# exp(scores) times V in a graph-attention layer: each matmul made as two of 64 queries, in two column tiles

## The chip, the core and the metric

The kernel runs on one core of a Trainium2 chip, everything in 32-bit floating point. The metric is the device time of one execution in microseconds (us), the median of several runs. A core has a tensor engine (PE, whose weight loads the profile lists apart as PEld), a vector engine (DVE), a scalar engine (ACT), GpSimd (POOL) and a queue that issues transfers (SP). Matmuls write to PSUM, the memory that DVE and ACT read the results from.

## The reference

128 graphs of 128 nodes, 768 features, 12 heads of 64. Cut to what matters:

```python
h = jnp.maximum(_layernorm(x), 0.0)
q = _split_heads(h @ Wq + bq); k = _split_heads(h @ Wk + bk); v = _split_heads(h @ Wv + bv)
scores = jnp.einsum('bhqd,bhkd->bhqk', q, k) / jnp.sqrt(HD) + beta * adj_e
scores = jnp.where(adj_e > 0, scores, -9e15)
probs = softmax(scores, axis=-1)
out = x + jnp.einsum("bhqk,bhkd->bhqd", probs, v)      # b: 128 graphs; heads put side by side
```


## The kernel before, in words

The work goes in 32 groups G of four graphs. A group needs three projections, called slices: `qk0` (queries and keys of heads 0 to 5), `v`, and `qk1` (queries and keys of heads 6 to 11). A slice is made of 15 products (`product`, line 316 is its matmul), by a scheme of sums and differences of blocks that needs fewer products than the plain one. Each product is 4 matmuls in the code, of 128 stationary columns and 256 moving columns, accumulated in one of four PSUM banks a, b, c, d; in the trace each matmul of the code is two weight loads and two matmuls, so a product is a group of 8. The very first slice is made in the plain way (`plain_slice`, line 443).

Attention works on pairs of heads; `oc` (0 to 5) numbers the pair. `scores(G, oc)` (matmul in line 355) makes the scores of both heads for the group's four graphs, keys on the partitions, queries along the free dimension. Its matmuls contract over 64 partitions: head i = 0 uses partitions 0 to 63 and i = 1 uses 64 to 127, two row tiles of the tensor engine's array, and the innermost loop alternates between them. DVE then caps the scores and adds the bias (line 358), ACT takes exp (line 359), and the results stand in the tiles `es[G, oc, i]` (called e in the trace).

`attend(G, oc)` (line 379) multiplies them with V: for each half r of the group, two graphs g and two heads i, exp(scores) of a graph and head, 128 keys by 128 queries, is the stationary operand; the moving operand is V of that graph and head, 128 keys by 65 columns, whose 65th column is ones, so that the sum of each row comes along. The result, 128 queries by 65, goes into a PSUM tile `pa` (called av in the trace) that holds four of them. A call is 8 matmuls in the code, 16 in the trace. `weigh` (lines 364 to 370) divides by the sums on DVE, POOL adds x (line 383), and SP writes the result out.

Each engine carries out its instructions in the order in which they are written. That order is written by hand: `slice_of` makes the products one after the other and calls, after certain products, the functions of a list `todo`. `attention(G, u)` fills it for three pairs of heads:

```python
for i in range(3):
    todo.setdefault(1 + 4 * i, []).append(lambda oc=3 * u + i: scores(G, oc))
    todo.setdefault(5 + 4 * i, []).insert(0, lambda oc=3 * u + i: attend(G, oc))
```

so scores stand after products 1, 5 and 9, attends after 5, 9 and 13, and after products 5 and 9 attend comes directly ahead of the next scores. Pairs 0 to 2 of a group are attended in its own `qk1` slice, pairs 3 to 5 in the next group's `qk0` slice. In the last group all six pairs have to be finished in its `qk1` slice: three calls of `attend` after products 3, 6 and 9, each followed by scores, and then six calls of `attend_half` (line 411), which do half the graphs each, directly behind calls of `scores_half` (line 397). All PSUM tiles of attention come from one ring of four banks (tag "at"), those of the products from another (tag "mm").

The kernel ends with a test of ranges (line 579 is its matmul), on which a second, plain computation (`general`) depends that isn't taken here.

Of the kernel before, what the change touches and what calls it, by code (L numbers as in the profile page):

```python
# [16 lines left out]
P = 128  # L17
# [89 lines left out]
def direct(ctx, tc, x, adj, wq, bq, wk, bk, wv, bv, beta, out, bad):  # L107
# [10 lines left out]
    nc = tc.nc  # L118
    B, N, D = x.shape
    HD = D // HEADS  # L120
# [17 lines left out]
    xg, A, biasT, vt, qk = {}, {}, {}, {}, {}  # L138
# [204 lines left out]
    es, xo = {}, {}  # L343
# [17 lines left out]
    def weigh(G, oc, r, pa, o):  # L361

        sm = stat.tile([P, 4, 1], F32, tag="sm", name=f"sm_{G}_{oc}_{r}")
        nc.vector.tensor_scalar(sm, pa[:, :, HD:VE], TINY, None, op0=ALU.max)
        rs = stat.tile([P, 4, 1], F32, tag="rs", name=f"rs_{G}_{oc}_{r}")
        nc.vector.reciprocal(rs, sm)
        nc.vector.tensor_mul(o, pa[:, :, 0:HD], rs.to_broadcast([P, 4, HD]))  # L367
        for i, t in enumerate((sm, rs)):
            s = seen[:, i, 4 * r:4 * r + 4]
            nc.vector.tensor_tensor(s, s, t.rearrange("p b e -> p (b e)"), ALU.max)  # L370

    def attend(G, oc):
        o = work.tile([P, 2, 4, HD], F32, tag="o", name=f"o_{G}_{oc}", bufs=2)
        for r in range(2):
            pa = psum.tile([P, 4, VE], F32, tag="at", name=f"av_{G}_{oc}_{r}")
            for g in range(2):
                for i in range(2):
                    h = 2 * oc + i
                    nc.tensor.matmul(pa[:, 2 * g + i, :], es[G, oc, i][:, 2 * r + g, :],  # L379
                                     vt[G, "v", r, h // 4][:, 4 * g + h % 4, :], start=True, stop=True)  # L380
            weigh(G, oc, r, pa, o[:, r])
        t = xo[G, oc]
        nc.gpsimd.tensor_add(t, t, o.rearrange("p a (b j) d -> p (a b) (j d)", j=2))  # L383
        nc.sync.dma_start(out[G * GRP:(G + 1) * GRP, :, oc * P:(oc + 1) * P].rearrange("g n d -> n g d"), t)
# [20 lines left out]
    def attend_half(G, oc, r):  # L405
        o = work.tile([P, 4, HD], F32, tag="o", name=f"o_{G}_{oc}_{r}", bufs=2)
        pa = psum.tile([P, 4, VE], F32, tag="at", name=f"av_{G}_{oc}_{r}")
        for g in range(2):
            for i in range(2):
                h = 2 * oc + i  # L410
                nc.tensor.matmul(pa[:, 2 * g + i, :], es[G, oc, r][:, i, g, :],  # L411
                                 vt[G, "v", r, h // 4][:, 4 * g + h % 4, :], start=True, stop=True)
        weigh(G, oc, r, pa, o)
        t = xo[G, oc, r]
        nc.vector.tensor_add(t, t, o.rearrange("p (b j) d -> p b (j d)", j=2))
        g0 = G * GRP + 2 * r
        nc.sync.dma_start(out[g0:g0 + 2, :, oc * P:(oc + 1) * P].rearrange("g n d -> n g d"), t)

    def attention(G, u):

        todo = {}
# [3 lines that stand above are left out]
        return todo  # L425
# [72 lines left out]
    for G in range(NG):  # L498
# [64 lines left out]
        for at, f, *args in (  # L563
            (0, scores, 0), (3, attend, 0), (3, scores, 1), (6, attend, 1), (6, scores, 2), (9, attend, 2),
            (9, scores_half, 5, 0), (10, scores_half, 4, 0), (11, attend_half, 5, 0), (12, scores_half, 3, 0),
            (12, attend_half, 4, 0), (13, scores_half, 3, 1), (13, attend_half, 3, 0), (14, scores_half, 5, 1),
            (14, attend_half, 3, 1), (14, scores_half, 4, 1), (14, attend_half, 5, 1), (14, attend_half, 4, 1),
        ):
            then(at, lambda f=f, args=args: f(G, *args))
# [143 lines left out]
```

## Time and profile before

| | |
|---|---|
| median of three runs | 3119.64 us (3119.45 to 3120.21) |
| profiled execution | 3119.99 us |
| its span, first to last instruction | 3118.2 us |
| granted clock of the tensor engine | 0.999 |
| HBM traffic | 54 GB/s over the span |

A row of the profile's groups names the line, the engine, the operation, the output and input tiles, for the tensor engine the rows and columns of the array in use (128*128, or 64*128 for the scores), the shape, and the count; then the busy time in us and the mean duration of one in ns, and last the idle time of the engine ahead of them. A busy time counts overlapping instructions once, and a matmul's duration holds its way through the array, so it is longer than the step from one matmul to the next. In the timeline, rows of equal instructions are merged: start, duration of the whole, engine, line, operation, tiles, shape and count. A row of one line's instructions gives the least, the median and the largest duration in ns.

### The profile page before, as it was taken

The page shows a single profiled execution, that of the slowest core. Times are in us where ns is not written, and L with a number is a line of the kernel's source. Part 1 is how long each engine was busy: PE and PEld are TensorE (multiplying, and loading weights), DVE is VectorE, ACT ScalarE, POOL GpSimd, SP SyncE. Part 2 cuts the span into 40 slices and gives each one's busy share as a digit, 9 for nine tenths or more (in the row PEclk, how much of TensorE's full clock was granted, in tenths as well). Part 3 has the DMA queues.
Part 4 walks back from the last instruction along what each step waited for, and adds up shares of the span by engine and source line. Part 5 has one row for each costly group of instructions (what it writes and reads, how often), then busy time and mean ns, then how long its engine had stood idle before and what let it go on. Part 6 is the DMA issues. An engine that isn't in the chain of part 4 may idle for free.

```text
span 3118.2 us, 46382 instructions
## 1 busy us (share of the span) xinstructions
PE 3099.8 (99%) x17846; PEld 2748.6 (88%) x17846; DVE 2000.8 (64%) x5155; ACT 801.1 (26%) x1703; POOL 375.8 (12%) x307
## 2 busy tenths in 40 slices
PE   8999999999999999999999999999999999999999
PEld 7888888888888888888888888888888888888887
DVE  7866656666566665666656666556666566665654
ACT  2222222322222222222232222222322222222221
POOL 1111111011110111111111111111011110111110
PEclk9999999999999999999999999999999999999999
DMA  5212112121122121221112212112121122111111
GB/s 154 72 48 58 41 48 65 52 54 46 44 65 58 48 55 42 57 62 49 54 40 56 65 48 58 41 48 65 52 55 44 46 65 57 49 52 40 56 35 38
DMA packets 358481, 169.94 MB, mean 54 GB/s; under 512 B 84464, under 2 KB 358128, under 8 KB 358256
## 3 DMA queue, kind: packets, MB, share of 16 engines
q1 hardware_dynamic: 355392, 166.14, 19.4%
q8 instruction: 142, 2.33, 0.3%
q10 hardware_dynamic: 2864, 0.79, 0.1%
q14 instruction: 83, 0.68, 0.1%
HBM read 116.53 MB, written 50.33 MB: 54 GB/s over the span
## 4 chain that ended last, share of the span: by engine, by line
PE 98%; DVE 1%; DMA 0%; ACT 0%; issue 0%; SPq 0%; ACTq 0%; DVEq 0%
PE pc_qk L316 18%; PE pb_qk L316 14%; PE pa_qk L316 14%; PE av L379 10%; PE pc_v L316 9%; PE pb_v L316 7%; PE pa_v L316 7%; PE pd_qk L316 7%; PE sc L355 7%; PE pd_v L316 4%; PE plain L443 1%; DMA x<-in_x_dram 0%; ACT x L259 0%; DVE A L266 0%; PE av L411 0%; PE pm L228 0%
## 5 line engine op out<-in xcount | busy, mean ns | idle before, releaser
L383 POOL TENSOR_TENSOR xo<-xo,o 128x512 f32<-128x512 f32 x189 | 258.3, 1367 | 2427.1 <-DVE seen L370 1496.1
L359 ACT ACTIVATE e<-e 128x512 f32<-128x512 f32 x378 | 231.9, 630 | 752.3 <-DVE e L358 751.6
L259 ACT ACTIVATE x<-x,shift,rstd 128x192 f32<-128x192 f32 x512 | 228.0, 533 | 588.3 <-POOL shift L250 588.3
L379 PEld LDWEIGHTS av<-v,e 128*128 128x128 f32 x3024 | 367.4, 192 | 9.8
L316 PE MATMUL pb_qk<-S,qk_T 128*128 128x256 f32 x1512 | 367.1, 386 | 0.0
L379 PE MATMUL av<-v,e 128*128 128x65 f32 x3024 | 358.2, 272 | 0.0
L337 ACT ACTIVATE qk<-pc_qk,bqk 128x256 f32<-128x256 f32 x378 | 158.1, 469 | 727.6 <-PE pc_qk L316 727.6
L358 DVE SCALAR_TENSOR_TENSOR e<-sc,biasT 128x512 f32<-128x512 f32 x378 | 243.0, 685 | 127.0 <-PE sc L355 127.0
L316 PEld LDWEIGHTS pb_qk<-S,qk_T 128*128 128x128 f32 x1512 | 277.3, 190 | 40.1
L341 DVE TENSOR_TENSOR qk<-qk,pb_qk 128x512 f32<-128x512 f32 x252 | 172.1, 683 | 162.9 <-PE pb_qk L316 144.7
L316 PE MATMUL pc_qk<-S,qk_B 128*128 128x256 f32 x1008 | 244.7, 386 | 1.2 <-ACT qk L337 1.2
L316 PE MATMUL pa_qk<-S,qk_T 128*128 128x256 f32 x1008 | 244.8, 386 | 0.0
L316 PE MATMUL pc_qk<-S,qk_T 128*128 128x256 f32 x1008 | 238.1, 379 | 0.0
L266 DVE STREAM_TRANSPOSE A<-x 128x256 f32<-128x256 f32 x384 | 217.4, 612 | 7.4 <-ACT x L259 7.3
L355 PE MATMUL sc<-qk 64*128 64x128 f32 x3024 | 219.6, 285 | 0.0
L316 PEld LDWEIGHTS pc_qk<-S,qk_T 128*128 128x128 f32 x1008 | 191.5, 190 | 26.0
L316 PEld LDWEIGHTS pc_qk<-S,qk_B 128*128 128x128 f32 x1008 | 186.3, 190 | 31.9 <-ACT qk L337 1.6
L316 PEld LDWEIGHTS pa_qk<-S,qk_T 128*128 128x128 f32 x1008 | 186.2, 190 | 30.5
L355 PEld LDWEIGHTS sc<-qk 64*128 64x128 f32 x3024 | 183.4, 187 | 29.5 <-issue 20.9
L316 PE MATMUL pb_v<-v_T,S 128*128 128x256 f32 x768 | 183.9, 382 | 0.0
L341 DVE TENSOR_TENSOR qk<-qk,pd_qk 128x512 f32<-128x512 f32 x126 | 86.6, 688 | 147.3 <-PE pd_qk L316 147.3
L367 DVE TENSOR_TENSOR o<-av,rs 128x256 f32<-128x256 f32 x384 | 160.3, 418 | 2.3 <-DVE seen L370 0.4
(117 smaller groups left out, 4516.1 us busy)
## 6 DMA issues: line engine op xcount, KB each, us to landing
x<-in_x_dram SPq DMA_DIRECT2D x504, 96.0 KB, 2.4
xo<-in_x_dram SPq DMA_DIRECT2D x189, 256.0 KB, 2.8
out_dram<-xo SPq DMA_DIRECT2D x189, 256.0 KB, 2.2
adj<-in_adj_dram SPq DMA_DIRECT2D x128, 64.0 KB, 2.3
qk_T<-in_L_gnn_Wq_dram SPq DMA_DIRECT2D x10, 128.0 KB, 3.2
qk_T<-in_L_gnn_Wk_dram SPq DMA_DIRECT2D x10, 128.0 KB, 3.1
v_T<-in_L_gnn_Wv_dram SPq DMA_DIRECT2D x5, 256.0 KB, 5.7
qk_B<-in_L_gnn_Wq_dram SPq DMA_DIRECT2D x8, 128.0 KB, 3.1
```

Source lines behind the costliest of these rows:

```text
L259: nc.scalar.activation(t, t, AF.Relu, bias=shift[G, n], scale=rstd[G, n])
L266: last = nc.vector.transpose(t[:, :, g * N:(g + 1) * N].rearrange("p c (b i) -> p c b i", i=SQ), src)
L316: nc.tensor.matmul(p[:, i, :], lhs, rhs, start=(first and i == 0 and c == 0), stop=(c == 1), skip_group_check=True)
L337: nc.scalar.activation(t[:, i, :], p[:, i, :], AF.Identity, bias=bqk[:, i, oc:oc + 1], scale=float(sign))
L341: added[G] = nc.vector.tensor_tensor(t, t, p, ALU.add if sign > 0 else ALU.subtract)
L355: nc.tensor.matmul(ps[i][:, g, :], t[r, 1, at], t[r, 0, at], start=True, stop=True)
L358: nc.vector.scalar_tensor_tensor(e, ps[i], SCORE_CAP * ISCALE, biasT[G], op0=ALU.min, op1=ALU.add)
L359: nc.scalar.activation(e, e, AF.Exp, scale=1.0 / ISCALE)
L367: nc.vector.tensor_mul(o, pa[:, :, 0:HD], rs.to_broadcast([P, 4, HD]))
L379: nc.tensor.matmul(pa[:, 2 * g + i, :], es[G, oc, i][:, 2 * r + g, :], vt[G, "v", r, h // 4][:, 4 * g + h % 4, :], start=True, stop=True)
L383: nc.gpsimd.tensor_add(t, t, o.rearrange("p a (b j) d -> p (a b) (j d)", j=2))
L443: nc.tensor.matmul(p[:, i, :], b[:, c, i * P:(i + 1) * P], a[:, c, :], start=(k == 0 and i == 0 and c == 0), stop=(c == 1), skip_group_che ...
```

## The change

In `attend` and `attend_half` each matmul becomes two, for queries 0 to 63 and 64 to 127 (`P` is 128, `HD` is 64). The stationary operand of each has 64 columns; the output goes to partitions 0 to 63 or 64 to 127 of the same PSUM tile, which puts the matmul on columns 0 to 63 or 64 to 127 of the array, two column tiles with all 128 rows each. The moving operand, V with 65 columns, is the same for both.

```diff
                 for i in range(2):
                     h = 2 * oc + i
-                    nc.tensor.matmul(pa[:, 2 * g + i, :], es[G, oc, i][:, 2 * r + g, :],
-                                     vt[G, "v", r, h // 4][:, 4 * g + h % 4, :], start=True, stop=True)
+                    for q in range(0, P, HD):
+                        nc.tensor.matmul(pa[q:q + HD, 2 * g + i, :], es[G, oc, i][:, 2 * r + g, q:q + HD],
+                                         vt[G, "v", r, h // 4][:, 4 * g + h % 4, :], start=True, stop=True)
             weigh(G, oc, r, pa, o[:, r])
```

The edit in `attend_half` is the same, with `es[G, oc, r][:, i, g, q:q + HD]` as the stationary operand.

More of the change, by code (lines that the diff above doesn't have):

```diff
@@ L410, in attend_half @@
                 h = 2 * oc + i
-                nc.tensor.matmul(pa[:, 2 * g + i, :], es[G, oc, r][:, i, g, :],
-                                 vt[G, "v", r, h // 4][:, 4 * g + h % 4, :], start=True, stop=True)
+                for q in range(0, P, HD):
+                    nc.tensor.matmul(pa[q:q + HD, 2 * g + i, :], es[G, oc, r][:, i, g, q:q + HD],
+                                     vt[G, "v", r, h // 4][:, 4 * g + h % 4, :], start=True, stop=True)
         weigh(G, oc, r, pa, o)
```

## The prediction, made before the change was run

> **What bounds the kernel now.** I read the page from the top: the busy times, then the chain of work that ended last, then the costliest groups, and after that the waits of the tensor engine.
>
> ```profile
> span 3118.2 us, 46382 instructions
> PE 3099.8 (99%) x17846; PEld 2748.6 (88%) x17846; DVE 2000.8 (64%) x5155; ACT 801.1 (26%) x1703; POOL 375.8 (12%) x307
> PEclk9999999999999999999999999999999999999999
> PE 98%; DVE 1%; DMA 0%; ACT 0%; issue 0%; SPq 0%; ACTq 0%; DVEq 0%
> L379 PEld LDWEIGHTS av<-v,e 128*128 128x128 f32 x3024 | 367.4, 192 | 9.8
> L379 PE MATMUL av<-v,e 128*128 128x65 f32 x3024 | 358.2, 272 | 0.0
> L355 PE MATMUL sc<-qk 64*128 64x128 f32 x3024 | 219.6, 285 | 0.0
> ```
>
> The tensor engine (PE) runs without a gap at its full clock, and the chain is PE for 98%. The other engines are never what ends last, so a microsecond taken from PE is a microsecond off the end, until some engine behind it falls late. The waits of PE say how near that is:
>
> ```profile
> engine line waited for: us in total, times, longest us
> PE pm L228 <- DVE st L219: 7.2, 2, 5.8
> ...
> PE pc_qk L316 <- ACT qk L337: 1.2, 1, 1.2
> ```
>
> The two largest lines are shown; all waits together are 13.4 us of 3118, and most of them stand at the start. The change touches the two groups named av: 3024 weight loads and 3024 matmuls, 16 of each per call of attend (each matmul of the code is two instructions in the trace), so 189 calls, and a matmul with 65 moving columns. What sets the pace inside such a call is read from the timeline of PE and of its weight loads (PEld). Columns: start, duration, engine, line, count.
>
> ```profile
> 1532.68 1.89 PE L316 MATMUL pa_qk<-S,qk_T 128*128 128x256 f32 x8
> 1534.40 1.90 PE L379 MATMUL av<-v,e 128*128 128x65 f32 x16
> 1536.23 1.16 PE L355 MATMUL sc<-qk 64*128 64x128 f32 x16
> 1537.32 1.99 PE L316 MATMUL pc_qk<-S,qk_B 128*128 128x256 f32 x8
> 1539.15 1.89 PE L316 MATMUL pb_qk<-S,qk_T 128*128 128x256 f32 x8
> ...
> 1554.26 1.90 PE L379 MATMUL av<-v,e 128*128 128x65 f32 x16
> 1555.99 0.43 PE L316 MATMUL pb_qk<-S,qk_T 128*128 128x256 f32 x1
> ```
>
> ```profile
> 1532.46 1.70 PEld L316 LDWEIGHTS pa_qk<-S,qk_T 128*128 128x128 f32 x8
> 1534.19 1.97 PEld L379 LDWEIGHTS av<-v,e 128*128 128x128 f32 x16
> ```
>
> ```profile
> L379 PE MATMUL av<-v,e x3024: 220/275/275, 87.2 to 3090.6; 128*128 128x65 f32 x189
> L316 PE MATMUL pc_qk<-S,qk_T x1008: 379/379/379, 75.6 to 3072.4; 128*128 128x256 f32 x168
> ```
>
> A product's 8 matmuls of 256 columns hold PE for 1.72 to 1.73 us until the next group (1532.68 to 1534.40), 0.216 us each, and their loads, which begin 0.22 us ahead of the matmuls they serve, vanish under the matmul before. The streaming price of a column comes from the shortest durations in the last fence: (379 - 220) / (256 - 65) = 0.83 ns, so 65 columns stream in 54 ns. Yet 16 av matmuls hold PE for 1.73 us until the next group (1554.26 to 1555.99). Their 16 loads take 1.97 us from first start to last end; the first lies under the product's last matmul, 0.216 us ahead of the second, and the 14 steps that are left make (1.97 - 0.19 - 0.216) / 14 = 0.112 us from load to load. So av is bound by its weight loads: 128 columns of exp(scores) take 0.112 us, and the 54 ns of streaming lie under the next load. The median av matmul is 275 ns against 220: 55 ns of waiting for weights, the other half of 0.112.
>
> **The load of 64 columns.** The trace has one load of another width, the last matmul of the kernel with one column:
>
> ```profile
> L579 PEld LDWEIGHTS pf<-over,ones x2: 79/80/82, 3112.3 to 3112.3; 128*1 128x1 f32 x2
> ```
>
> 192 - 80 = 112 ns for 127 columns more, 0.88 ns a column: 64 columns fewer shorten a load by 56 ns, to 56 ns of pace. Half of 0.112 says the same. The matmul beside it, 54 ns of streaming plus 3 ns (0.216 us of L316 less 256 x 0.83 ns), has a pace of 57 ns. I take p = 0.058 us for one load and one matmul on one column tile, the larger plus the trace's 10 ns rounding over the block.
>
> **Do two tiles run at once?** No column tile is in this trace; the nearest row is the scores, which use two row tiles (64*128). Their 16 matmuls stream 128 columns, 128 x 0.83 = 106 ns each, with a load of 128 columns each, 0.112 us. One after the other would be 1.79 us; from 1536.23 to 1537.32 they take 1.09 us, and that contains a change of mode. Between the ends stand: full overlap, p = 0.058 us for each pair of tiles, and none, 2 x 0.058 = 0.116 us. I take full overlap, since the row tiles show it in fp32, with the same alternation of tiles from one matmul to the next as the new inner loop over q, and since the two new matmuls write different partitions of a bank.
>
> On this the Trainium skill, page "TensorE: Matmul & The Clock Gate", section "Part 3: Packing small matmuls — row/col tiling", gives a measured 2.38 times for three column tiles. My estimate from that page is 2.38 / 3 x 2 = 1.59 for two, hence p = 0.112 / 1.59 = 0.070 us, and a total of 3040 us by the formula below; no run here shows it.
>
> **The change of mode, which is added.** Between full-array matmuls and the scores PE changes its tiling. What that costs is read from starts: a product takes 8 x 0.216 = 1.73 us, but
>
> ```profile
> 1524.48 1.89 PE L316 MATMUL pa_qk<-A,qk_T 128*128 128x256 f32 x8
> 1526.30 1.16 PE L355 MATMUL sc<-qk 64*128 64x128 f32 x16
> 1527.39 1.99 PE L316 MATMUL pb_qk<-S,qk_T 128*128 128x256 f32 x8
> 1529.22 1.89 PE L316 MATMUL pc_qk<-S,qk_T 128*128 128x256 f32 x8
> ```
>
> the product ahead of the scores holds PE for 1.82 us: 0.09 us in which the array empties. The product behind them has 1.99 instead of 1.89 us and lasts 1.83: 0.10 us in which its first load stands exposed. The scores themselves close: 0.10 exposed + 8 x 0.112 + 0.09 = 1.09 us, the measured value. So a mode change costs 0.09 us plus the first load; for a 64-column load I take half, 0.05 us.
>
> **The sum for one call of attend.** Today, from its first matmul to the next group's: 1.83 us where the scores follow (1534.40 to 1536.23), 1.73 us where a product follows, and there the product's first matmul has 0.05 us of waiting for weights (0.43 against 0.38 us), so 1.78. Afterwards: 0.09 to empty the array ahead of it (new, since a product comes before), 0.05 for the first load, 16 p = 0.93 for 16 pairs, 0.09 to empty it again, 1.16 us together. The scores behind it pay for their exposed load today already. A product behind it now pays 0.10: 1.26.
>
> So 0.67 us are saved where the scores follow and 0.52 where a product follows. The order is the same for every slice of attention: attends at places 5, 9 and 13, scores at 1, 5 and 9, so two calls of three are followed by scores. The last group's first three (LAST) are all followed by scores. That gives 62 calls with a product behind and 127 with scores, 189 in all. 127 x 0.67 + 62 x 0.52 = 117 us. As a formula in p, for use below: saved = 127 (1.60 - 16 p) + 62 (1.45 - 16 p) = 293 - 3024 p, with 118 us at p = 0.058 (the difference is rounding).
>
> The six half calls at the end (L411) are taken at nothing: 48 instructions, at most 48 x 0.054 = 2.6 us, in a tail where exp ends some of the waiting.
>
> **What could be late next.** attend reads exp(scores), which the vector and scalar engines finish well before:
>
> ```profile
> 1538.11 1.28 DVE L358 SCALAR_TENSOR_TENSOR e<-sc,biasT 128x512 f32<-128x512 f32 x2
> 1538.88 1.23 ACT L359 ACTIVATE e<-e 128x512 f32<-128x512 f32 x2 [3.44 <-DVE e L358]
> ...
> 1526.00:1587.00 61.00, 61.00 (x384) 54.13 (x383) 42.65 (x117) 17.04 (x35) 7.36 (x6) 1.00 0.23 66
> ```
>
> The av that reads these tiles starts four products later, and exp ends at 1540.11, when one of the four products has passed (1537.32 to 1539.15) and the second has run 0.96 us; over 4 us remain, and the products that carry this margin are unchanged. In the stretch of attention slices (third line: PE, PEld, DVE, ACT, POOL) DVE has 42.65 of 61 us; with six calls less 0.6 us each, 42.65 of 57.2, 75%. No queue gains an instruction but PE's (3072 loads and 3072 matmuls more), no DMA is added, and no semaphore wait by the code. If DVE's cover went, each bank handed back late would cost PE its length; nothing in the waits of PE points there.
>
> The profiled execution took 3119.99 us, 1.8 beyond its span; the runs shown have a median of 3119.64. 3119.99 - 118 = 3002 us.
>
> **Rivals.** *The tiles take turns.* If the loads of both column tiles pass one path into the array, a pair costs 2 x 0.058 = 0.116 us, no more than 128 columns cost today, and the mode changes are pure loss: 293 - 3024 x 0.116 = -58, 3178 us. It decides from p = 293 / 3024 = 0.097 us on. For it: both tiles read the same 128 partitions, while the row tiles of the scores read disjoint ones. Against it: loads and matmuls already read the same partitions at once (PEld 1532.46 under PE). 0.10.
>
> *A load may not pass a matmul of the other tile.* Then a pair is 0.058 of loading and 0.057 of streaming in turn, 0.115 us: 3175 us. The trace speaks against the mechanism where it can be seen, since the L316 loads run under matmuls of the same 128 rows; it has no case with tiles on the same rows. 0.06. The Trainium skill has this rule, in the same section of "TensorE: Matmul & The Clock Gate": a load overlaps matmuls in flight only if its row group differs, and the two column tiles have the same rows. By that rule the change would lose; the L316 rows above disagree with it in its plain form.
>
> *Instructions come too slowly.* The densest stretch today is the scores, 32 instructions in 8 x 0.112 us, 0.028 us each; the new call wants 0.0145. Held to 0.028, a pair with its four instructions costs 0.112: 3166 us. Nothing shows 0.028 to be a limit, because the loads set that pace by themselves. 0.02.
>
> *No tiling happens.* The narrow matmuls run one after the other in the full array, without mode changes: 32 x 0.058 against 16 x 0.112, 0.07 us more per call, 189 x 0.07 = 13, 3133 us. For it: the label 128*1 of the last load names the columns in use, not a tile. Against it: the row tiles came from the operands' partitions alone. 0.05.
>
> *Break-even*, p near 0.097 within 0.002: 0.03.
>
> **How the numbers follow.** Full overlap 0.74, the others 0.26. 0.2% of the time is 6 us, about what a measurement of this kernel can tell from no change; only the break-even case lies inside it. Faster 0.74, same 0.03, slower 0.10 + 0.06 + 0.02 + 0.05 = 0.23. The likeliest case's own range: below, if entering the column tiles needs no emptying (189 x 0.09 = 17 us) nor leaving them for a product (62 x 0.09 = 6): 2980. Above, if a mode change with column tiles costs twice as much (189 x 0.14 + 62 x 0.19 = 38 us): 3040, and 3045 with some late banks. The whole range reaches on to the untiled case, 2980 to 3135, and leaves out the three serial ones, 0.18.
>
> **What would show it.** In the changed profile the av rows should read 128*64 with 6048 of each kind, loads of about 136 ns. A call should run 1.0 us in the timeline, with starts of matmuls in pairs; the next group begins 1.07 us after the first av matmul, and the product ahead lasts 1.82 us. The chain stays PE for 98%, with av near 6%. A call of about 2 us means turns or a limit of issue; a call of 1.8 us with no 0.09 us ahead of it means no tiling; calls of 1.1 us with a saving far under 118 us mean that DVE became late, to be seen as waits of PE for L332, L341 or L367. The prediction is wrong if p is over 0.072 us.

## The result, and the profile after

The changed kernel takes 3007.57 us (median of four runs, 3005.77 to 3007.84) against 3119.86 us before (3119.45 to 3120.21, four runs). The ratio is 0.9639, 95% interval 0.9622 to 0.9656: 112 us less, where 118 were forecast. The page of the profile after, with the rows that answer to those of before:

```profile
span 3006.0 us, 52526 instructions
...
PE 2985.7 (99%) x20918; PEld 2579.4 (86%) x20918; DVE 1996.6 (66%) x5155; ACT 797.3 (27%) x1703; POOL 359.7 (12%) x307
...
PE 98%; DVE 1%; DMA 0%; ACT 0%; issue 0%; SPq 0%; ACTq 0%; DVEq 0%
...
L380 PEld LDWEIGHTS av<-v,e 128*64 128x64 f32 x6048 | 192.6, 138 | 62.9 <-issue 43.0
...
L380 PE MATMUL av<-v,e 128*64 128x65 f32 x6048 | 218.8, 225 | 0.0
```

PE still fills 99% of the span, and the chain is PE for 98%: no other engine became the bound. The av rows read 128*64, so the tiles were made, with twice the instructions (6048) in 219 instead of 358 us of busy time. A load of 64 columns takes 138 ns against 192, near the 136 that the one-column load had led to expect. A matmul's mean is 225 ns against 272: close to the 220 ns that it takes without a wait, so the waiting for weights is nearly gone. The idle time ahead of these loads grew from 9.8 to 62.9 us, which is 0.33 us in each of the 189 calls: the first load of a call, which started 0.21 us ahead of its matmul before (1534.19 and 1534.40), now starts together with it (both 1483.19 below), 0.09 us after the product ahead has had its 1.73.

The timeline of PE after shows two calls with what stands around them, the first followed by scores, the second by a product. Columns: start, duration, engine, line, count.

```profile
1481.37 1.89 PE L316 MATMUL pa_qk<-S,qk_T 128*128 128x256 f32 x8
1483.19 1.16 PE L380 MATMUL av<-v,e 128*64 128x65 f32 x32
1484.27 1.16 PE L355 MATMUL sc<-qk 64*128 64x128 f32 x16
1485.37 2.00 PE L316 MATMUL pc_qk<-S,qk_B 128*128 128x256 f32 x8
```

```profile
1440.37 1.89 PE L316 MATMUL pa_qk<-S,qk_B 128*128 128x256 f32 x8
1442.19 1.15 PE L380 MATMUL av<-v,e 128*64 128x65 f32 x32
1443.27 2.00 PE L316 MATMUL pb_qk<-S,qk_T 128*128 128x256 f32 x8
1445.10 1.89 PE L316 MATMUL pc_v<-v_T,S 128*128 128x256 f32 x8
```

Ahead of av the product now holds PE for 1.82 us in place of 1.72, the added change of mode. The call itself takes 1.08 us to the next group's start; before it took 1.83 ahead of scores and 1.73 ahead of a product. Behind it the product now lasts 1.83 us (1443.27 to 1445.10), with its first load exposed. A row merges the matmuls of a group; their single starts, which the trace holds too, fall in 16 pairs in each of the 189 calls, the second of a pair 7 ns (median) behind the first. The waits of PE after:

```profile
engine line waited for: us in total, times, longest us
PE pm L228 <- DVE st L219: 7.1, 2, 5.8
PE pc_qk L316 <- ACT qk L337: 2.3, 1, 2.3
PE plain L445 <- DVE A L266: 2.0, 1, 2.0
PE pf L581 <- DVE over L578: 1.7, 1, 1.7
PE av L413 <- ACT e L404: 0.9, 2, 0.5
PE pm L243 <- DVE dev L235: 0.5, 1, 0.5
```

They add up to 14.5 us. Before, the six lines (7.2, 1.7, 1.6, 1.2, 0.5 and 0.2 us) make 12.4, and not the 13.4 of the prediction: 2.1 us more, in the first 97 us and at the end. Behind the longest of the waits that grew (2.3 us, up to 97.38), the clock granted to PE is 0.50 from about 98.8 to 102.2 us, which the profile before does not have. The call of `attend` there takes 1.93 us in place of 1.08. My estimate is 1.7 us of lost time, half of these 3.4.

### The profile page after: what moved, and what is told of

Its sections match the earlier page's. It is cut to its first block, busy times and chain, and to the rows that moved or that the text cites. A ratio compares the mean times of both kernels' runs of the same rounds, so it can differ in the third digit from the quotient of the medians.

```text
span 3006.0 us, 52526 instructions
## 1 busy us (share of the span) xinstructions
PE 2985.7 (99%) x20918; PEld 2579.4 (86%) x20918; DVE 1996.6 (66%) x5155; ACT 797.3 (27%) x1703; POOL 359.7 (12%) x307
## 4 chain that ended last, share of the span: by engine, by line
PE 98%; DVE 1%; DMA 0%; ACT 0%; issue 0%; SPq 0%; ACTq 0%; DVEq 0%
PE pc_qk L316 18%; PE pb_qk L316 15%; PE pa_qk L316 15%; PE pc_v L316 9%; PE pb_v L316 7%; PE pa_v L316 7%; PE pd_qk L316 7%; PE av L380 7%; PE sc L355 7%; PE pd_v L316 4%; PE plain L445 1%; DMA x<-in_x_dram 0%; ACT x L259 0%; DVE A L266 0%; DVE qk_T L199 0%; PE pm L228 0%
## 5 line engine op out<-in xcount | busy, mean ns | idle before, releaser
L384 POOL TENSOR_TENSOR xo<-xo,o 128x512 f32<-128x512 f32 x189 | 242.1, 1281 | 2330.5 <-DVE seen L370 2300.9
L380 PEld LDWEIGHTS av<-v,e 128*64 128x64 f32 x6048 | 192.6, 138 | 62.9 <-issue 43.0
L380 PE MATMUL av<-v,e 128*64 128x65 f32 x6048 | 218.8, 225 | 0.0
L272 DVE TENSOR_TENSOR S<-A,A 128x512 f32<-128x512 f32 x224 | 164.2, 747 | 1.0
```

The costliest lines, as they stand in the source:

```text
L272: nc.vector.tensor_tensor(t, A[G, a], A[G, b], ALU.add if sign > 0 else ALU.subtract)
L380: nc.tensor.matmul(pa[q:q + HD, 2 * g + i, :], es[G, oc, i][:, 2 * r + g, q:q + HD], vt[G, "v", r, h // 4][:, 4 * g + h % 4, :], start=Tru ...
```

## The experiments

The theory on trial: two column tiles work at once, so a call has 16 steps of 0.058 us instead of 16 of 0.112, and it pays for an added change of mode. A mode is the way in which the array is divided into tiles: 128*128, 64*128 or 128*64 in the rows. The rivals: the gain comes from narrow loads as such, or changes of mode cost nothing or something else than they were priced at.

**Blocks of eight.** The two tiles get the same instructions, in blocks and no longer in turn (in `attend`; the half calls at the end stay).

```diff
-            for g in range(2):
-                for i in range(2):
-                    h = 2 * oc + i
-                    for q in range(0, P, HD):
+            for q in range(0, P, HD):
+                for g in range(2):
+                    for i in range(2):
+                        h = 2 * oc + i
```

> The changed kernel with the loop over the two column tiles outermost: for each PSUM tile first all four matmuls on columns 0 to 63, then all four on columns 64 to 127. The same instructions, shapes and changes of mode. Theory (two tiles run at once, but matmuls start in the order written, so tiles overlap only where they alternate): the tiles overlap only at the three places of a call where the tile changes, so a call has 32 - 3 = 29 steps of 0.058 us in place of 16, 0.75 us more in each of 189 calls: about 3150 us. Rival (the gain comes from the narrow loads, or the engine finds the other tile's matmul by itself): no change, 3008 us.

Measured: 3079.83 us, ratio to before 0.9873 (0.9853 to 0.9893). From the timeline of this kernel:

```profile
1515.38 1.55 PE L380 MATMUL av<-v,e 128*64 128x65 f32 x32
1516.86 1.16 PE L355 MATMUL sc<-qk 64*128 64x128 f32 x16
```

A call takes 1.48 us against 1.08, with the same 32 narrow loads and matmuls. The rival "narrow loads alone" falls: the order in which the tiles come is worth 72 us. But the theory's size was wrong too: it gave about 3150 us. A step of the changed kernel is (1.08 - 0.14) / 16 = 0.0588 us, where 0.14 is the first load and the emptying, so a call in blocks has (1.48 - 0.14) / 0.0588 = 22.8, that is 23 steps, and 9 of them must hold two of the 32 matmuls, where strict order allows 3. The single starts in the trace say the same: in each of the 189 calls they fall on 23 moments, 9 of them with two starts. So a matmul can start ahead of waiting ones of the other tile.

**Blocks of sixteen, and of four.** Two kernels were to tell how far ahead: all 16 instructions of one tile first (both PSUM tiles of the call, then the divisions), and blocks of four (both heads of a graph).

```diff
+        pas = [psum.tile([P, 4, VE], F32, tag="at", name=f"av_{G}_{oc}_{r}") for r in range(2)]
+        for q in range(0, P, HD):
+            for r in range(2):
+                for g in range(2):
+                    for i in range(2):
...
+        for r in range(2):
+            weigh(G, oc, r, pas[r], o[:, r])
```

```diff
-                for i in range(2):
-                    h = 2 * oc + i
-                    for q in range(0, P, HD):
+                for q in range(0, P, HD):
+                    for i in range(2):
+                        h = 2 * oc + i
```

> As e1_blocked with longer blocks: all 16 instructions of a call on columns 0 to 63 first, over both PSUM tiles, then all 16 on columns 64 to 127. e1_blocked had blocks of 8 and showed 9 overlapped steps of 32 (1.48 us a call in place of 1.08) where starts in order allow 3. Theory A (a matmul may start ahead of about 4 waiting ones of the other tile): only the last 4 of the first block overlap, 28 steps, a call of 1.76 us, 0.68 us more than in the changed kernel: about 3136 us. Theory B (starts strictly in order): 31 steps, 3170 us. Theory C (the engine finds the other tile's work at any distance within its queue of instructions): 3008 us, or at most 3080 us like e1_blocked. In all of them the divisions of the first half start later, under matmuls that follow.

> As e1_blocked with shorter blocks: for each graph the matmuls of both heads on columns 0 to 63 (4 instructions), then both on columns 64 to 127. Theory A (a reach of about 4 waiting instructions): the blocks overlap nearly in full, 16 to 17 steps, 3008 to 3020 us. Theory B (starts strictly in order): one overlapped step at each of 7 changes of tile, 25 steps in place of 16, 0.52 us a call more, 3107 us.

Measured: 3145.00 us with blocks of sixteen, ratio 1.0081 (1.0061 to 1.0101), and 3016.13 us with blocks of four, ratio 0.9668 (0.9649 to 0.9688). The timelines, sixteen first:

```profile
1546.33 1.90 PE L380 MATMUL av<-v,e 128*64 128x65 f32 x32
1548.16 1.16 PE L355 MATMUL sc<-qk 64*128 64x128 f32 x16
```

```profile
1485.97 1.20 PE L380 MATMUL av<-v,e 128*64 128x65 f32 x32
1487.11 1.16 PE L355 MATMUL sc<-qk 64*128 64x128 f32 x16
```

1.83 us are (1.83 - 0.14) / 0.0588 = 28.7, that is 29 steps, and 1.14 us are 17; the single starts fall on 29 and on 17 moments in every call. One rule gives all three counts: a matmul may start ahead of up to three waiting matmuls of the other tile. With blocks of sixteen, 13 steps hold one matmul, 3 hold two and 13 hold one, 29 in all. With blocks of eight it is 5 + 3 + 2 + 3 + 2 + 3 + 5 = 23, the threes with two each. With blocks of four only the first and the last run alone, 17.

The reach of 3 (4 was guessed) is fitted to these calls, and the trace doesn't name the tile of an instruction. Yet that matmuls pass one another can be seen in it. The matmul that tells DVE that the first PSUM tile is complete is the 16th of a call in the order of writing, and in the changed kernel it is the 16th to start. With blocks of eight it is the 19th to start, in each of the 189 calls, so three written behind it went ahead. The first matmul of a block can be told too, by its exposed load (0.27 us in place of 0.22): written 9th, 17th and 25th, it starts 6th, 14th and 22nd. That each engine carries out its instructions in the order in which they are written, as was said ahead of the prediction, is thus too strict for PE. What the three kernels also show is what no overlap would cost: with 26 of 32 matmuls alone, the same column tiles make the kernel slower than before, 3145 us, not far from the 3178 that was worked out for none.

**One half in tiles.** The half r = 0 of `attend` stays at full width.

```diff
-                    for q in range(0, P, HD):
-                        nc.tensor.matmul(pa[q:q + HD, 2 * g + i, :], es[G, oc, i][:, 2 * r + g, q:q + HD],
+                    M = HD if r else P
+                    for q in range(0, P, M):
+                        nc.tensor.matmul(pa[q:q + M, 2 * g + i, :], es[G, oc, i][:, 2 * r + g, q:q + M],
```

> In attend the half r = 0 keeps the full-width matmuls of the kernel before, the half r = 1 has the two column tiles (the calls of attend_half stay with tiles). Theory (a change into column tiles costs 0.14 us, one out of them 0.09 us and the next group's exposed load): a call is 8 x 0.112 + 0.09 + 0.05 + 8 x 0.058 + 0.09 = 1.60 us, against 1.83 (scores behind) and 1.78 (product behind, which then pays 0.10 more): 127 x 0.23 + 62 x 0.08 = 34 us saved, about 3085 us. Rival (changes of mode are free and the gain goes with the number of matmuls): half of the 112 us, 3064 us. Rival (most of the price is paid by the first matmuls of the tiles): over 3095 us.

Measured: 3074.16 us, ratio 0.9854 (0.9838 to 0.9871). The timeline of PE:

```profile
1514.34 1.62 PE L381 MATMUL av<-v,e 128*128 128x65 f32 x24
1515.89 1.16 PE L355 MATMUL sc<-qk 64*128 64x128 f32 x16
```

The number alone does not decide: 3074 lies midway between the theory's 3085 and the 3064 of free changes of mode. The call does. It takes 1.55 us where 1.60 were expected. The full-width half had been given 8 x 0.112 us, but its first load lies under the product ahead, so its 8 matmuls end 0.05 us sooner. 0.05 x 189 = 9 us is the difference to 3085, within 2 us. With free changes a call would save half of what the whole change saves. It saves 45 us and not 56: so a price is paid once for each call, and is no share of its matmuls.

**Four tiles of 32 queries.** `HD` becomes 32 (`SQ`) in the loop over q and in the slices, in `attend` and in `attend_half`.

```diff
-                    for q in range(0, P, HD):
-                        nc.tensor.matmul(pa[q:q + HD, 2 * g + i, :], es[G, oc, i][:, 2 * r + g, q:q + HD],
+                    for q in range(0, P, SQ):
+                        nc.tensor.matmul(pa[q:q + SQ, 2 * g + i, :], es[G, oc, i][:, 2 * r + g, q:q + SQ],
```

> Four column tiles of 32 queries in place of two of 64. Theory (with two tiles the load of 64 columns, 0.056 us, and the streaming of 65 columns, 0.057 us, are tied; with four the load falls to 0.028 and streaming sets the pace): a step stays at 0.057 us, the first exposed load is 0.025 us shorter, the four tiles start 0.007 us apart: 3000 to 3008 us. Rival (instructions are issued no faster than the 4 in 0.058 us that the changed kernel shows): 8 instructions take 0.117 us, a call 0.93 us more, about 3184 us. Rival (loads alone set the pace): a step of 0.03 us, a call 0.45 us less, about 2925 us.

Measured: 3000.91 us (3000.61 to 3002.71), ratio 0.9620 (0.9603 to 0.9636). The group of loads, and a call in the timeline:

```profile
L380 PEld LDWEIGHTS av<-v,e 128*32 128x32 f32 x12096 | 181.3, 110 | 62.7 <-issue 42.8 <-ACT qk L337 19.9
```

```profile
1480.54 1.12 PE L380 MATMUL av<-v,e 128*32 128x65 f32 x64
1481.60 1.16 PE L355 MATMUL sc<-qk 64*128 64x128 f32 x16
```

128 instructions in 1.06 us are 0.008 us each, so the rival of slow issue falls: the 0.028 us of the scores and the 0.0145 of two tiles were no limits. The load fell to 110 ns and the call only from 1.08 to 1.06 us: in the trace the four matmuls of a step start 0.007 us apart, and a new step begins every 0.057 us, the time of 65 streamed columns, and with two tiles the step was 0.0585. So streaming paces a step now, and at two tiles load and stream were nearly level, as the prediction had them (0.056 and 0.057 us). The narrower tiles bring 6.7 us more, and by the same reading still narrower ones would bring next to nothing; that was not tried.

**Fewer changes of mode.** The order of the calls in the 62 slices that `attention` fills:

```diff
-        for i in range(3):
-            todo.setdefault(1 + 4 * i, []).append(lambda oc=3 * u + i: scores(G, oc))
-            todo.setdefault(5 + 4 * i, []).insert(0, lambda oc=3 * u + i: attend(G, oc))
+        for at, f, i in ((1, scores, 0), (1, scores, 1), (6, attend, 0), (6, attend, 1), (8, scores, 2), (12, attend, 2)):
+            todo.setdefault(at, []).append(lambda f=f, oc=3 * u + i: f(G, oc))
```

> The changed kernel with another order in the 62 slices of attention that attention() fills: scores of pairs 0 and 1 after product 1, attends 0 and 1 after product 6, scores 2 after product 8, attend 2 after product 12. No instruction more or less; changes of the tensor engine's tiling per slice fall from 10 to 8 (one change into scores, 0.09 us and an exposed load of 0.10, and one into the column tiles, 0.09 and 0.05, less). Theory (mode changes are what is lost, nothing else falls late): 0.33 us x 62 = 20 us off, 2987 us. Rival (mode changes cost nothing by themselves): 3008 us. Rival (the vector engine, which gets two calls' divisions at once, hands banks back late): waits of the tensor engine appear, 3008 us or more.

Measured: 2985.71 us (2985.31 to 2988.40), ratio 0.9572 (0.9556 to 0.9587), the expected 20 us and two more. The timeline:

```profile
1466.75 2.06 PE L355 MATMUL sc<-qk 64*128 64x128 f32 x32
1468.73 1.99 PE L316 MATMUL pb_qk<-S,qk_T 128*128 128x256 f32 x8
...
1475.74 1.89 PE L316 MATMUL pc_qk<-S,qk_B 128*128 128x256 f32 x8
1477.56 2.09 PE L380 MATMUL av<-v,e 128*64 128x65 f32 x64
1479.58 1.99 PE L316 MATMUL pb_qk<-S,qk_T 128*128 128x256 f32 x8
```

Two calls of scores take 1.98 us together in place of 2 x 1.09, two attends 2.02 in place of 2 x 1.08. That is 0.20 and 0.14 us in each slice, x 62 = 21 us. The products around them pay as before: four in a slice are 0.09 us longer ahead of a change of mode and four 0.10 us longer behind one, in either order.

The next kernel puts scores 2 directly behind the two attends: `(7, attend, 0), (7, attend, 1), (7, scores, 2), (13, attend, 2)`.

> As e4_pairs, but scores 2 directly behind the two attends (after product 7) and attend 2 after product 13: 7 changes of tiling per slice in place of 10 (one into scores, one into column tiles and one into products less, 0.19 + 0.14 + 0.19 us). Theory: 0.52 x 62 = 32 us off, 2975 us. Rival (the four PSUM banks of attention run out: scores 2 need the banks of attend 0, whose divisions the vector engine has not finished when attend 1 ends): about 1 us of waiting per slice, to be seen as waits of PE at sc for o or sm, 3030 us or so.

Measured: 3018.98 us, ratio 0.9679 (0.9663 to 0.9695). The rival was right. In its timeline the scores behind two attends stretch, although one mode change less stands in the slice:

```profile
1494.48 2.09 PE L380 MATMUL av<-v,e 128*64 128x65 f32 x64
1496.70 1.74 PE L355 MATMUL sc<-qk 64*128 64x128 f32 x16
1498.38 1.99 PE L316 MATMUL pd_qk<-A,qk_T 128*128 128x256 f32 x8
```

In this slice they start 2.22 us behind the first av matmul in place of 2.02, and hold PE for 1.68 in place of 1.09. The late start is found in 30 of the 62 slices only, once as much as 6.29 us, and the other 32 start on time; the stretch is in all. Added up over the trace it is 10 us of late starts and 36 of stretching, 46 us, which takes 2975 to 3021, near the time measured. The list of waits names only the longest (4.2 us, sc for DVE at L370). The timeline of DVE shows what the others are for. In this slice its divisions (L367) of the two halves of attend 0 end at 1496.56 and 1497.17; the first scores matmul starts at 1496.70 and the first one of the second head at 1497.32, 0.14 and 0.15 us later. By the ring of four, these two halves hold the banks that the scores get next. More banks were not tried.

To see whether column tiles have anything to do with the gain of pairs, the order was given to the kernel before as well:

> The kernel before, full-width matmuls of exp(scores) with V, in the order of e4_pairs: per slice one change of tiling into the scores and one out of them less (0.19 us each), none of column tiles. Theory (mode changes cost 0.09 us and the exposed load, whatever the tiles): 0.38 us x 62 = 24 us off, 3096 us. Rival (the gain of e4_pairs came from the vector engine's work being spread otherwise, or from the column tiles): 3119 us.

Measured: 3102.20 us (3101.57 to 3103.58), ratio 0.9944 (0.9928 to 0.9961). That is 17.7 us less than the kernel before, where the theory had 24 and the rival 0. Grouping gains without column tiles too, but less than was worked out. Its timeline:

```profile
1528.96 3.68 PE L379 MATMUL av<-v,e 128*128 128x65 f32 x32
1532.48 1.95 PE L316 MATMUL pb_qk<-S,qk_T 128*128 128x256 f32 x8
```

Two attends hold PE for 3.52 us in place of 2 x 1.83, 0.14 us less, and two calls of scores for 1.99 in place of 2 x 1.09, 0.19 less. Against that, the product that now stands behind the attends lasts 1.79 us in place of 1.73: full-width av leaves the load behind it exposed by 0.06 us even without a change of mode. So a slice gains 0.14 + 0.19 - 0.05 = 0.28 us, with the rounding of the rows, and not 0.38; 0.28 x 62 = 17 us.

**Both together**, four tiles in the order of pairs:

> Four column tiles of 32 queries (e3_quarters) in the order of e4_pairs. Theory (shorter calls and fewer mode changes add up, nothing else falls late): 3007.6 - 6.7 - 21.9 = 2979 us. Rival (the vector engine is late behind two calls at once, now still shorter): no better than e4_pairs, 2986 us or more.

Measured: 2980.03 us (2979.68 to 2981.21), ratio 0.9554 (0.9538 to 0.9570): the sum holds, and this kernel beats both the one before and the changed one.

## Why the prediction was right

*The bound.* A call was paced by its loads of 128 columns, 0.112 us each, and PE was the end of everything. Both held: PE lost 114 us of busy time and the span 112.

*The pace p.* 0.058 us for a pair of tiles at work together was the step on which the sign hung. From the rows after, (1.08 - 0.05 - 0.09) / 16 = 0.059 us. The experiments show that it is overlap, not narrowness: the same instructions in blocks lose up to 137 us. The prediction had taken overlap over from the row tiles of the scores, by analogy, and named the alternation of tiles as what the two have in common; the blocks show that the gain does hang on it, beyond a reach of three matmuls.

*The changes of mode.* 0.09 us ahead of av was forecast and is there (1481.37 to 1483.19, 1.82 us). The call was to take 1.07 us and takes 1.08; the row itself reads 1.15 to 1.16 and not 1.0, since it lasts to the end of the last matmul.

*The sum.* By the medians over all calls of the two traces, a call ahead of scores saves 1.825 - 0.093 - 1.083 = 0.649 us (forecast 0.67). One ahead of a product saves 0.506 (forecast 0.52): the call and the product behind it took 1.731 + 1.782 us before and take 1.083 + 1.831 now, and the product ahead is 0.093 longer. 127 x 0.649 + 62 x 0.506 = 114 us, 4 less than forecast. These are two hundredths of a microsecond in each call, of which 0.007 us are the step by which the second tile starts behind the first, which the working left out, and 0.01 are 16 steps of 0.0585 in place of 0.058. The rest of the difference stands outside the sum: 1.5 us of longer waits up to 97 us, about 1.7 for the stretch at half the clock, and on the other side 1.3 us saved in the tail with the six half calls (3090.83 to 3112.26 us before, 2979.89 to 3000.00 after), which had been taken at nothing. Together they give 112.

*The rivals.* That the tiles take turns falls with the pairs of starts 7 ns apart; blocks of sixteen come near its time (3145 us) because most of their matmuls run alone. The rule of the Trainium skill ("TensorE: Matmul & The Clock Gate", Part 3) that a load overlaps matmuls in flight only if the row group differs gave 3175 us: here both tiles have the same rows and 3007.6 was measured, so for this case the rule does not hold. From the 2.38 times that the Trainium skill gives in the same section for three tiles, 3040 us had been estimated, which was too much: the step went from 0.112 to 0.0585 us, 1.9 times where the estimate had 1.59. The statement of the Trainium skill in that section that matmuls start strictly in order doesn't hold for the blocks either, where the 16th matmul written is the 19th to start. Issue was no limit down to 0.008 us an instruction.

## What to carry to other kernels

When the profile shows a matmul with few moving columns at a pace that equals its weight load (here 0.112 us for 128 columns of weights, against 0.054 us of streaming), the load is the bound. Splitting the stationary operand into column tiles then lets its parts load at the same time, if consecutive matmuls alternate between the tiles or nearly so (blocks of four lost 8.6 us here, blocks of sixteen more than the whole gain). Count the changes of tiling mode before and after: 0.09 us of emptying and an exposed first load each, which are read from the starts of the groups around a mode that the kernel has already, and grouping calls of one mode wins part of it back (22 us here) until a call has to wait for the banks of the one before (33 us lost again). Stop splitting where the load has fallen to the streaming time.

## What the runs showed of the hardware beyond that

PE keeps four column tiles busy with 128 instructions in 1.06 us. The order of writing matters less than expected: blocks of four cost 8.6 us, blocks of eight 72 and blocks of sixteen 137 over strict alternation, and in all three a matmul starts ahead of three that wait for the other tile. And a product behind full-width av takes 1.78 to 1.79 us in place of 1.73 without any change of mode, so moving a call of scores away from there saves less than a whole change.
